# Projecting P and Q in two halves of TensorE's rows, and moving the places of nodes into a tile of differences

## The chip, the core and the metric

The kernel runs on one core of one Trainium2 chip. It is one program in one launch. The metric is the device time of that launch in microseconds (us), the median of several runs. The engines go by the names of the profile: PE (TensorE, with PEld for its weight loads), DVE (VectorE), ACT (ScalarE), POOL (GpSimd) and SP (SyncE, which issues the DMAs).

## What is computed

128 small graphs of 128 nodes with 64 features go through four residual layers, each after a layer norm and a maximum with zero. Almost all of the time goes to layer 0, a message over the edges:

```python
mask = (adj > 0.0).astype(x.dtype)
W1a, W1b = (W1[:F], W1[F:])
xj_proj = x @ W1a
diff = x[:, :, None, :] - x[:, None, :, :]
h = jax.nn.relu(xj_proj[:, :, None, :] + diff @ W1b + b1)
hm = jnp.einsum('bjkh,bjk->bjh', h, mask)
deg = jnp.sum(mask, axis=-1)
return hm @ W2 + deg[..., None] * b2
```

Here F is 64 and the hidden width H0 is 192. About an eighth of the entries of adj is not zero, and every node has an edge to itself. Layer 1 is three graph convolutions and an output projection, layer 2 is one convolution whose rows are normalized and then scaled by a mean and a variance over all nodes of all graphs, and layer 3 is a convolution followed by a small two-layer network.

## The kernel before

**Layer 0 as gathers.** For an edge from j to k the hidden value is relu(P[j] + Q[k]), where P = h (W1a + W1b) + b1 and Q = -h W1b. The kernel projects P and Q once for each node and then, instead of going over all 128 x 128 pairs, goes over the neighbours of each node: the i-th neighbour of all nodes in one task. Q is split into three bf16 parts whose sum is the fp32 value, and a one-hot matrix (`oh`, `ohn`) picks the rows of Q by matmuls that add onto P, which lies in PSUM already.

**Groups and pairs.** Four graphs (G) make a group, so there are 32 groups (NG). Two graphs (a pair p of NP = 2) share the 128 partitions when they are transposed: hT has 64 rows of features of the one and 64 of the other. Before the change the weights wp and wq are block diagonal, 128 rows by 2 x 192 columns with zeros in the off-diagonal blocks, so that one matmul of 128 rows and 384 columns projects both graphs of a pair. W is 384.

**Tasks.** A group has 20 tasks in layer 0 (ORDER). A near task (4 matmuls of 192 columns) covers one of three thirds of the nodes with all three parts of Q at once, a full task (12 matmuls) covers one neighbour of all nodes. The three tiles blk0 to blk2 in PSUM take turns: task t uses block t % 3. In each task `fill` copies P of the group into a block (ACT, L560), `differences` adds Q on PE (tile name blk), and DVE adds the positive part to acc (L583; the first tasks of a group are L579 and L581). `fill(t + 2)` and the one-hot of task t + 3 are written down after the first quarter of task t.

**PSUM.** There are eight banks. Each blk has two, of which columns 0 to 383 hold P and differences; 128 columns of each bank are spare. The spare columns hold ysum (blk0), ysq (blk1) and the degrees of nodes (`degs_at`, blk2), all set to zero at the start. The remaining two banks are the pool ps, from which `bank(name)` takes one in turn for everything else.

**Side work.** Between the half tasks of group g, two generators are advanced: `prepare(g + 1)` and `after_layer0(g - 1)`, which is `layer0_end` (tiles ps_sA, ps_sB, ps_o), `layer1` (ps_ah, ps_ag, ps_pr, t at L640) and `layer2_norm` (ps_ga, ps_pr, y at L654, sqy at L656, nrm). A planner in `network` chooses: each half task allows PACE us of PE work, by the estimate of `spend`, and a generator that lags behind its schedule by LAG steps runs anyway. N_PREPARE and N_AFTER are the numbers of steps. The framework then orders each engine's instructions, mostly as they are written down, with ready ones first, and adds the waits. It keeps two engines from one PSUM bank at a time by waits.

**prepare(g)**, in its order: transposed adjacency; ranks of neighbours (ps_rank, ps_rankT, leftT at L424); keys and `lower` (L441); the place of each node in an order by the number of its neighbours, from matmuls into ps_place, read by `to_b` (L452); hT (L328); Q (ps_q, the copies L465, the subtractions L466, the casts L467 and L468, the DMAs to q_dram and back into near_q); hs, the features in the new order (ps_ga); num (L482); degrees into degs_at, read by spare_n (L510); fro (L495); P (ps_p with its bias, copied to psort at L517), psort_r by DMA, and extra (L525).

All matmuls are recorded at L103, the transposes at L108, so the tile names tell them apart.

## Time and profile before

| | |
|---|---|
| runs | 1396.9, 1397.42 and 1404.55 us, median 1397.42 |
| profiled execution | 1398.05 us, its span 1396.2 |
| mean granted clock of TensorE | 0.979 |
| PE busy | 1232.2 us (88%) |
| DVE busy | 1167.8 us (84%) |
| ACT busy | 990.8 us (71%) |
| POOL busy | 270.6 us (19%) |
| ps_p, fp32 matmul passes | 128 records, 59.0 us busy |
| ps_q, fp32 matmul passes | 128 records, 52.5 us busy |

The span is the time from the first to the last instruction of one profiled execution. A busy time is the sum over which at least one instruction of the engine runs; matmuls are pipelined, so each lasts longer in the records than it keeps the next one off, and the spacing of their starts says more than their lengths. "Idle before" is the time in which an engine stood still ahead of a group of instructions, with the instruction that ended it. The chain is followed back from the last instruction, at each step to what released it; a piece of work that is not on it can still take part in the next longest chain.

### The profile page before, as it was taken

The numbers are of one execution on the slowest core, as the hardware profiler recorded it, in microseconds if no ns is written. First come the engines' busy times: TensorE is split into PE (matmuls) and PEld (weight loads), VectorE is DVE, ScalarE is ACT, GpSimd is POOL, SyncE is SP. The second block draws the span as 40 slices with busy tenths as digits, with TensorE's granted clock in tenths as the row PEclk, the third lists the DMA queues.
The fourth block names the chain that finished last, engine by engine and source line by source line (L and its number), as shares of the span: only waits on it lengthen the run. The fifth ranks groups of instructions, "written<-read, shape, count | busy, mean of one in ns | idle before, by whom it ended". The sixth has DMA issues, their size and how long they took to land.

```text
span 1396.2 us, 29319 instructions
## 1 busy us (share of the span) xinstructions
PE 1232.2 (88%) x10964; PEld 959.3 (69%) x10964; DVE 1167.8 (84%) x2629; ACT 990.8 (71%) x1883; POOL 270.6 (19%) x322
## 2 busy tenths in 40 slices
PE   3788999999999999999999999999999999995787
PEld 1467777777777777777777777776777777763566
DVE  6898888888888888888888888888898888866973
ACT  1677777777777777777777777777777777753783
POOL 3111111111111111111111111111111111015830
PEclk9899999999999999999999999999999999997889
DMA  5443222322323222222222222223222212200345
GB/s 120 131 120 98 67 66 78 83 83 84 83 76 83 84 75 75 76 63 75 66 78 84 83 84 83 75 83 84 76 75 79 62 59 60 76 9 15 93 112 126
DMA packets 108788, 110.97 MB, mean 79 GB/s; under 512 B 42895, under 2 KB 88220, under 8 KB 108636
## 3 DMA queue, kind: packets, MB, share of 16 engines
q1 hardware_dynamic: 108636, 109.00, 28.5%
q8 instruction: 89, 1.46, 0.5%
q14 instruction: 63, 0.52, 0.1%
HBM read 52.70 MB, written 35.29 MB: 63 GB/s over the span
## 4 chain that ended last, share of the span: by engine, by line
PE 65%; ACT 17%; DVE 13%; issue 2%; SPq 1%; DMA 1%; DVEq 0%; POOL 0%; ACTq 0%; POOLq 0%
PE blk L103 24%; PE ps_pr L103 10%; ACT blk L560 9%; DVE acc L583 6%; PE ps_ag L103 5%; PE ps_p L103 5%; PE ps_sA L103 5%; PE ps_o L103 3%; PE ps_sB L103 3%; PE ps_q L103 2%; PE ps_ah L103 2%; PE ps_hm L103 2%; ACT q L465 2%; DVE leftT L424 1%; PE ps_key L103 1%
## 5 line engine op out<-in xcount | busy, mean ns | idle before, releaser
L583 DVE SCALAR_TENSOR_TENSOR acc<-blk,acc 128x768 f32<-128x768 f32 x576 | 543.1, 950 | 65.0 <-PE blk L103 38.9
L560 ACT COPY blk<-psort 128x768 f32<-128x768 f32 x544 | 436.1, 806 | 134.1 <-DVE acc L583 132.2
L103 PE MATMUL blk<-q,oh 128*128 128x192 bf16 x3072 | 318.2, 246 | 34.5 <-ACT blk L560 34.3
L103 PEld LDWEIGHTS <-oh 128*128 128x128 bf16 x3072 | 259.1, 98 | 89.3 <-issue 84.3
L103 PE MATMUL blk<-near_q,ohn 128*128 128x192 bf16 x1536 | 199.7, 246 | 22.4 <-ACT blk L560 22.1
L103 PEld LDWEIGHTS <-ohn 128*128 128x128 bf16 x1536 | 134.7, 98 | 59.9 <-issue 45.3
L468 POOL TENSOR_TENSOR q<-rest,q 128x768 bf16<-128x768 f32 x32 | 52.8, 1648 | 209.1 <-ACT q L467 209.1
L642 POOL TENSOR_TENSOR adjT<-adjT,ident 128x512 f32<-128x512 f32 x32 | 41.9, 1310 | 254.8 <-PE ps_ag L103 254.8
L668 POOL TENSOR_TENSOR y<-y,nrm 128x256 f32<-128x256 f32 x32 | 19.7, 615 | 363.7 <-PE blk L103 238.1
L634 ACT COPY msg<-ps_pr 128x512 f32<-128x512 f32 x64 | 37.5, 586 | 68.9 <-PE ps_pr L103 67.5
L541 DVE TENSOR_SCALAR ohn<-near_n 128x1536 bf16<-128x1536 bf16 x128 | 84.3, 695 | 0.0
L103 PE MATMUL ps_pr<-g,dT 128*128 128x128 f32 x512 | 78.8, 288 | 0.8 <-ACT dT L626 0.8
L560 ACT COPY blk<-psort_r 128x768 f32<-128x768 f32 x96 | 77.5, 807 | 0.5 <-DVE acc L583 0.4
L103 PEld LDWEIGHTS ps_pr<-g,dT 128*128 128x128 f32 x512 | 64.3, 191 | 11.5 <-issue 7.2
L103 PE MATMUL ps_ag<-adjT,msg 128*128 128x128 f32 x512 | 71.5, 283 | 0.6 <-ACT msg L634 0.5
L103 PEld LDWEIGHTS <-ones_b 3*128 3x128 bf16 (+2 forms) x280 | 26.0, 93 | 59.1 <-issue 51.5
L103 PEld LDWEIGHTS ps_ag<-adjT,msg 128*128 128x128 f32 x512 | 62.1, 191 | 5.9 <-ACT msg L634 5.5
L103 PE MATMUL ps_p<-wp,hs 128*128 128x384 f32 x128 | 59.0, 543 | 0.0
L626 ACT ACTIVATE dT<-ps_ag 128x512 f32<-128x512 f32 x96 | 56.8, 592 | 3.0 <-PE ps_ag L103 2.8
L103 PE MATMUL ps_q<-wq,hT 128*128 128x384 f32 x128 | 52.5, 534 | 4.4 <-ACT hT L328 0.8
L103 PE MATMUL ps_hm<-ident,h 128*64 128x128 f32 x248 | 43.6, 308 | 14.0 <-ACT h L841 13.9
L103 PE MATMUL ps_sA<-fro,acc 128*128 128x128 f32 x256 | 53.3, 290 | 2.1 <-ACT dT L626 1.9
(220 smaller groups left out, 2544.8 us busy)
## 6 DMA issues: line engine op xcount, KB each, us to landing
q_dram<-q SPq DMA_DIRECT2D x32, 567.0 KB
near_q<-q_dram SPq DMA_DIRECT2D x96, 189.0 KB
near_n<-n_dram SPq DMA_DIRECT2D x96, 126.0 KB
a<-in_adj_dram SPq DMA_DIRECT2D x32, 256.0 KB
adjT_dram<-adjT SPq DMA_DIRECT2D x32, 256.0 KB
adjT<-adjT_dram SPq DMA_DIRECT2D x32, 256.0 KB
psort_r<-psort SPq DMA_DIRECT2D x32, 228.0 KB
fro_r<-fro SPq DMA_DIRECT2D x32, 152.0 KB
```

The lines of the kernel that those rows point to most:

```text
L103: return nc.tensor.matmul(o, w, x, **kw)
L424: nc.vector.scalar_tensor_tensor(flat(leftT), pk, float(NEAR), flat(mT), ALU.is_gt, ALU.mult)
L465: nc.scalar.copy(parts_q[:, 0, p, :], pq[:, 0:W])
L468: nc.gpsimd.tensor_tensor(parts_q[:, 2], rest, parts_q[:, 1], ALU.subtract)
L541: nc.vector.tensor_scalar(oh.rearrange("p t b n -> p (t b n)"), near_n[g % 2].rearrange("p t b n -> p (t b n)"), float(i + 1), None, ALU.i ...
L560: nc.scalar.copy(columns(t), psorts[g][in_segments(n)])
L583: nc.vector.scalar_tensor_tensor(acc, o, 0.0, acc, ALU.max, ALU.add)
L626: nc.scalar.activation(flat(dT), pa, AF.Relu)
L634: nc.scalar.copy(flat(msg), pm)
L642: nc.gpsimd.tensor_tensor(adjT, adjT, ident.unsqueeze(1).to_broadcast([P, G, P]), ALU.add)
L668: nc.gpsimd.tensor_tensor(y, y, over_f(nrm), ALU.mult)
```

## The change

P and Q are now projected by `projected`. wp and wq hold the same 64 x 192 weights twice, once in each half of the rows, without the zero blocks. Each fp32 matmul has 64 rows and 192 columns: half k of hT (or hs) against half k of the weights, into bank k, so that one bank holds the first graphs of both pairs and the other the second ones. `issue_after` fixes that the two halves alternate on PE. Both banks of the pool are taken at once. For P the two bias matmuls (3 rows, 384 columns) come first, one for each bank. The copies take one bank each, of the same size as before, with another layout of the destination; they all follow the matmuls at once, and the two steps that the pairs had become one step that counts as two.

The places of a group come into spare columns of blk1 (`places_at`) in place of a bank of their own; they are added onto the zeros set at the start. ysq leaves blk1: it takes the columns of the degrees in blk2, set to zero anew after the last group. The two memsets of the padded weights on POOL go. `spend` counts fp32 matmuls of 64 rows at half, and PACE goes from 0.85 to 0.82. The diff, without the blank lines that it adds:

```diff
--- before.py
+++ after.py
@@ -46,7 +46,7 @@
 ORDER = [kind[sum(k is kind for k in ORDER[:n])] for n, kind in enumerate(ORDER)]
 FIRST, FIRST_R = 0, ORDER.index((None, FULL))
 N_PREPARE, N_AFTER = 14, 26
-PACE, LAG = 0.85, 2.5
+PACE, LAG = 0.82, 2.5
 LATE = 18
 LASTS = 1.9
 PARTS = [2, 4, 6, 6, 6, 8]
@@ -94,7 +94,7 @@
         f32 = dtype == F32
         kind = (f32, tuple(w.shape), n)
         m = w.shape[-1]
-        one = max(0.026, 0.00043 * n) if not f32 else max(0.22, 0.0018 * n) * (0.5 if m == F and n == P else 1.0)
+        one = max(0.026, 0.00043 * n) if not f32 else max(0.22, 0.0018 * n) * (0.5 if m == F and n == P or w.shape[0] == F else 1.0)
         spent["us"] += one + (0.045 if kind != spent["kind"] else 0.0)
         spent["kind"] = kind
 
@@ -160,13 +160,12 @@
 
     w1, w2 = io["L0_gnn_W1"], io["L0_gnn_W2"]
 
-    wp = keep.tile([P, 2, H0], F32, name="wp")
-    wq = keep.tile([P, 2, H0], F32, name="wq")
-    wtop = setup.tile([P, 2, H0], F32, tag="wtop", name="wtop")
+    wp = keep.tile([P, H0], F32, name="wp")
+    wq = keep.tile([P, H0], F32, name="wq")
+    wtop = setup.tile([P, H0], F32, tag="wtop", name="wtop")
     for t, src in ((wtop, w1[0:F, :]), (wp, w1[F : 2 * F, :])):
-        nc.gpsimd.memset(t, 0.0)
         for k in range(2):
-            nc.sync.dma_start(t[k * F : (k + 1) * F, k, :], src)
+            nc.sync.dma_start(t[k * F : (k + 1) * F, :], src)
     nc.vector.tensor_scalar(wq, wp, -1.0, None, ALU.mult)
     nc.vector.tensor_tensor(wp, wp, wtop, ALU.add)
     w2a = keep.tile([P, F], F32, name="w2a")
@@ -252,9 +251,9 @@
             matmul(t[:, k * 512 : (k + 1) * 512], ones_b[0:3, :], rows3[:, 0:512], start=True, stop=True)
 
 
-    ysum, ysq = (t.rearrange("p (a n) -> p a n", a=2)[0:G, :, W:512] for t in blks[0:2])
-    degs_at = blks[2].rearrange("p (a n) -> p a n", a=2)[:, :, W:512]
-    for t in (ysum, ysq, degs_at):
+    behind_blk = [t.rearrange("p (a n) -> p a n", a=2)[:, :, W:512] for t in blks]
+    ysum, places_at, degs_at = behind_blk[0][0:G], behind_blk[1], behind_blk[2]
+    for t in (ysum, places_at, degs_at):
         nc.vector.memset(t, 0.0)
 
 
@@ -391,6 +390,32 @@
         nc.scalar.copy(flat(adjT), pt)
         nc.sync.dma_start(saved[g], flat(adjT))
         return adjT
+    def few(t, g):
+        half, at = divmod(g, NG // 2)
+        return t[:, half, at * 2 * G : (at + 1) * 2 * G]
+    def projected(ht, w, name, bias_row=None):
+        both = [bank(name) for _ in range(2)]
+        last = None
+        for k in range(2) if bias_row else ():
+            with tc.issue_after(last.ins) if last is not None else ExitStack():
+                last = matmul(both[k][:, 0:W].rearrange("p (a h) -> p a h", a=NP), ones_b[0:3, :], bias(bias_row, NP), start=True, stop=False, skip_group_check=True)
+        for p in range(NP):
+            for k in range(2):
+                half = slice(k * F, (k + 1) * F)
+                with tc.issue_after(last.ins) if last is not None else ExitStack():
+                    last = matmul(both[k][:, p * H0 : (p + 1) * H0], ht[half, p, :], w[half, :], start=bias_row is None, stop=True, skip_group_check=True)
+        return [t[:, 0:W].rearrange("p (a h) -> p a h", a=NP) for t in both]
+    def graphs(t, k):
+        return t[:, :, k * H0 : (k + 1) * H0]
 
     sorts, psorts, accs, loaded = {}, {}, {}, {}
 
@@ -444,9 +469,9 @@
         nc.vector.scalar_tensor_tensor(flat(rank), flat(rank_t), float(NEAR), flat(rank), ALU.min, ALU.add)
         nc.vector.tensor_copy(degs[:, :, 1], prv[:, :, P - 1])
         yield
-        pl = bank("ps_place")
-        for b in range(G):
-            matmul(pl[:, b : b + 1], lower[:, b, :], ones_b[:, 0:1], start=True, stop=True)
+        pl = few(places_at, g)
+        for b in range(G):
+            matmul(pl[:, b : b + 1], lower[:, b, :], ones_b[:, 0:1], start=False, stop=True, skip_group_check=True)
         next(ln)
         to_b = once.tile([P, G, P], BF16, tag="to_b", name="to_b")
         nc.vector.tensor_tensor(to_b, row_b.unsqueeze(1).to_broadcast([P, G, P]), pl[:, 0:G].unsqueeze(2).to_broadcast([P, G, P]), ALU.is_equal)
@@ -458,12 +483,11 @@
         hT = transposed(h, "0")
         yield
         rest = once.tile([P, NP, W], F32, tag="rest", name="rest")
-        for p in range(NP):
-            pq = bank("ps_q")
-            matmul(pq[:, 0:W], hT[:, p, :], flat(wq), start=True, stop=True)
-            yield
-            nc.scalar.copy(parts_q[:, 0, p, :], pq[:, 0:W])
-            nc.vector.tensor_tensor(rest[:, p, :], pq[:, 0:W], parts_q[:, 0, p, :], ALU.subtract)
+        pq = projected(hT, wq, "ps_q")
+        for k in range(2):
+            nc.scalar.copy(graphs(parts_q[:, 0], k), pq[k])
+            nc.vector.tensor_tensor(graphs(rest, k), pq[k], graphs(parts_q[:, 0], k), ALU.subtract)
+        yield 2
         nc.scalar.copy(parts_q[:, 1], rest)
         nc.gpsimd.tensor_tensor(parts_q[:, 2], rest, parts_q[:, 1], ALU.subtract)
         nc.sync.dma_start(q_dram[g], parts_q[0 : 3 * THIRD].rearrange("n q p c -> n q (p c)"))
@@ -484,8 +508,7 @@
         for q in range(3):
             nc.sync.dma_start(near_n[g % 2][q * THIRD : (q + 1) * THIRD].rearrange("r t b n -> r t (b n)"), n_dram[g].rearrange("(t r) c -> r t c", t=3))
         yield
-        half, at = divmod(g, NG // 2)
-        pd = degs_at[:, half, at * 2 * G : (at + 1) * 2 * G]
+        pd = few(degs_at, g)
         for b in range(G):
             matmul(pd[:, 2 * b : 2 * b + 2], to_b[:, b, :], degs[:, b, :], start=False, stop=True, skip_group_check=True)
         pf = bank("ps_fro")
@@ -510,12 +533,10 @@
         nc.vector.scalar_tensor_tensor(spare_n[:, g], pd.rearrange("p (b q) -> p b q", q=2), -1.0, caps.unsqueeze(1).to_broadcast([P, G, 2]), ALU.mult, ALU.add)
         yield
         psort = edge.tile([P, NP, W], F32, tag="psort", name="psort")
-        for p in range(NP):
-            pp = bank("ps_p")
-            matmul(pp[:, 0:W].rearrange("p (k h) -> p k h", k=2), ones_b[0:3, :], bias("L0_gnn_b1", 2), start=True, stop=False)
-            matmul(pp[:, 0:W], hs[:, p, :], flat(wp), start=False, stop=True)
-            nc.scalar.copy(psort[:, p, :], pp[:, 0:W])
-            yield
+        pp = projected(hs, wp, "ps_p", "L0_gnn_b1")
+        for k in range(2):
+            nc.scalar.copy(graphs(psort, k), pp[k])
+        yield 2
         psort_r = once.tile([P, NP, W], F32, tag="psort_r", name="psort_r")
         for n, start in zip(SEGS, STARTS):
             nc.sync.dma_start(psort_r[start : start + n], psort[0:n])
@@ -768,6 +789,8 @@
         return bank(name) if i == 0 else blks[i - 1][:, k * 512 : (k + 1) * 512]
 
     run(last)
+    ysq = degs_at[0:G]
+    nc.vector.memset(ysq, 0.0)
     for g in range(NG):
         y = ys[g]
         nc.vector.tensor_tensor(y, y, over_g(shift), ALU.subtract)
```

## Prediction

> **What bounds the kernel now.** I read the page's busy line, the busy time of the regular middle, the chain that ended last by line and then in order of time, and the timeline around each edited step. Busy line, then the stretch from 200 to 1150 us:
>
> ```profile
> PE 1232.2 (88%) x10964; PEld 959.3 (69%) x10964; DVE 1167.8 (84%) x2629; ACT 990.8 (71%) x1883; POOL 270.6 (19%) x322
> 200.00:1150.00 950.00, 874.30 (x7796) 685.92 (x7794) 830.68 (x1766) 713.53 (x1343) 157.14 (x176) 1.00 0.27 76
> ```
>
> In the middle PE is busy 874.3 of 950 us (92%), DVE 87%, ACT 75%. PE leads, but DVE is near, and a cut in PE's work is worth its full length only where the chain runs on PE. The place step L452 returns every 37.6 us on average, so there are 31 such periods and a first group before them. Chain by engine and line, then one period of it in order of time:
>
> ```profile
> PE 65%; ACT 17%; DVE 13%; issue 2%; SPq 1%; DMA 1%; DVEq 0%; POOL 0%; ACTq 0%; POOLq 0%
> PE blk L103 24%; PE ps_pr L103 10%; ACT blk L560 9%; DVE acc L583 6%; PE ps_ag L103 5%; PE ps_p L103 5%; PE ps_sA L103 5%; PE ps_o L103 3%; PE ps_sB L103 3%; PE ps_q L103 2%; PE ps_ah L103 2%; PE ps_hm L103 2%; ACT q L465 2%; DVE leftT L424 1%; PE ps_key L103 1%
> ```
>
> ```profile
> 610.69 0.44 DVE t L640
> ...
> 614.39 0.93 PE ps_q L103 x2
> 615.34 0.48 ACT q L465
> ...
> 623.76 1.11 PE ps_p L103 x3
> 626.63 1.11 PE ps_p L103 x3
> ```
>
> The reader is to see three things. Both projections of P are whole on the chain, 2 x 1.11 us. Of Q only the first half is (0.93); from there until 621.51 the chain runs over ACT and DVE. And at 610.69 it goes through t, a DVE read that has nothing to do with what PE does next, except that it frees a PSUM bank.
>
> **P.** An fp32 matmul appears as two passes. The timeline of PE has one projection of P like this:
>
> ```profile
> 623.52 0.24 PE L103 MATMUL blk<-degs,to_b 128*128 128x2 bf16 x4
> 623.69 0.33 PE L103 MATMUL ps_p<-rows,ones_b 3*128 3x384 bf16 x1
> 623.95 0.91 PE L103 MATMUL ps_p<-wp,hs 128*128 128x384 f32 x2
> 624.70 0.82 PE L103 MATMUL blk<-near_q,ohn 128*128 128x192 bf16 x8
> ```
>
> From bias to projection 0.26 us pass, though a 384-column bf16 stream alone takes 0.16 (192 columns start 0.08 apart): a switch between 3-row and 128-row weights costs 0.10. The two passes need 0.75: 2 x 0.3225, the spacing of passes within ps_q, and 0.11 for a first weight load that nothing covers. With 0.10 for entering the 3-row mode: 1.11.
> After the change one group has an entry 0.10, two bias matmuls 0.32, a switch to 64 rows 0.10, a bare first load 0.11, eight passes of 192 columns (0.161 each) in two banks of rows, and a switch back 0.10. Side by side the passes take 4 x 0.161 = 0.645, in all 1.38 against 2.22: **-0.84**. The trace holds no 64-row matmul[...].
> Do the halves run side by side? The nearest row is the other split, by columns:
>
> ```profile
> 618.91 0.66 PE L103 MATMUL ps_ga<-to,h 128*64 128x128 f32 x8
> 619.50 0.40 PE L103 MATMUL ps_num<-to_b,rank 128*128 128x128 bf16 x4
> ```
>
> Eight passes and a switch in 0.59 us, where eight full-width passes of 128 columns (0.11) would need 0.86: two at a time. [...] By the row 0.645[...]. I take the row, since both cases are two tiles of fp32, and keep 0.20 (no overlap at all) and 0.84 as ends.
>
> **Q.** PE's time falls from 0.11 + 4 x 0.3225 = 1.40 to 0.96 (0.10 + 0.11 + 0.645 + 0.10; the entry falls into the wait for hT that is there now). The path does not get shorter: the first copy now needs both pairs of graphs of its half, which end after 0.11 + 0.645, just when the first pair ended before. ACT's two copies (0.48 each), DVE's two subtractions (0.55) and all later casts are the same in number and size. The copies now follow each other with no fill (L560, 0.80) between, so one fill comes 0.48 later and PE's next differences with it; the second fill comes when it did. The last cast, POOL's subtraction (1.65) and the four DMAs behind it on SP (q_dram, three near_q) move one step, some 0.94 us, later; no near_q DMA appears among the waits of the middle, so their cover is the rest of the group; without it they would cost those 0.94. **0**, ends -0.2 and +0.3.
>
> **Places.** Four matmuls and their reader to_b stay, but leave the ring of two free banks (tag ps) for blk1. Around them now:
>
> ```profile
> 610.49 0.24 PE L103 MATMUL ps_place<-ones_b,lower 128*128 128x1 bf16 x4
> 610.53 0.80 ACT L560 COPY blk<-psort 128x768 f32<-128x768 f32 x1 [2.29 <-DVE acc L583]
> 611.03 0.95 DVE L583 SCALAR_TENSOR_TENSOR acc<-blk,acc 128x768 f32<-128x768 f32 x1
> 611.17 0.49 PE L103 MATMUL ps_o<-w2b,sB 128*128 128x128 f32 x2 [0.44 <-DVE t L640]
> 611.90 0.68 DVE L452 TENSOR_TENSOR to_b<-row_b,ps_place 128x512 bf16<-128x512 bf16 x1
> ```
>
> ps_o waits 0.44 for t because the banks alternate: ps_pr, place, ps_o. With place gone, ps_o gets the bank that lower read long before: **-0.44**.
> [...] 20 tasks a group over 3 blocks rotate the place through the ring. If blk1 is the task about to start, to_b ends (612.58) as its matmuls start: 0. If it is the next one, the place waits for the fill until 611.33, and ps_o starts 0.43 later than now. If it is the one just read, it waits for the accumulation until 611.98: 1.08 later. [...] The trace has the same construction in the degrees in blk2; idle time before them:
>
> ```profile
>   ACT blk L560: 3.7, 9
> ```
>
> 3.7 us over 32 groups are 0.12 each, as other matmuls are queued ahead. But its reader takes 0.15 us and to_b 0.68. I take **+0.25**, nearer the row; ends 0.12 and 0.50. What queues behind a late place on PE is ps_o, and behind to_b on DVE the next mean and accumulation.
>
> **Two banks at once.** P and Q each hold both free banks until their copies are done. For Q both were in turn used by it before. For P, ps_pr (L2's) is in the way:
>
> ```profile
> 625.10 0.39 ACT L656 ACTIVATE sqy<-ps_pr 128x256 f32<-128x256 f32 x1
> ```
>
> Its bank is free at 625.5, 1.8 us after P starts now; the second bias, and by the written order everything of P, waits for it, and ps_ah (625.54) must then wait for a copy of psort. Eight differences (0.67) and twelve more (1.0) can fill PE meanwhile. Ends 0 and 1.7; the nearest row is the 0.44 of ps_o: **+0.45**.
>
> **Given back.** In the period from 642 the stretch behind P runs over ACT (fills, four extras of 0.45) for 7.8 us, as long as PE's own in the period shown. Where that holds, a part of P's gain meets ACT: **+0.15**, ends 0 and 0.4.
>
> **Rest.** Two POOL memsets (0.5 each) go; POOL has memsets until 11 us and the first x lands at 23, so 0. In the first group ps_q and ps_p are 2.93 each on the chain at a lower clock; about 1 each goes: -2 once. The memset of ysq goes to the end, beside the shift subtractions: 0. PACE asks for 0.82 instead of 0.85 us of PE work per half task, about what the projections save; it moves steps by a half task and I cost it at 0, ends -0.3 and +0.3.
>
> **Sum.** -0.84 - 0.44 + 0.25 + 0.45 + 0.15 = -0.43 us a group, times 31 is -13.3, with -2 makes -15. The profiled execution took 1398.05 us (span 1396.2), 0.6 above the median 1397.42; from the median: **1382**, own range 1366 to 1392.
>
> **Rivals.**
> All of it arrives (no bank wait, place at 0.12, nothing given back): -1.16 x 31 - 2 = -38, 1359. For it speaks the 65% of the chain on PE; against it DVE's 87%, which would become 90%.
> It is eaten: waits of 0.9 a group in place of one of 0.44, near 1397.
> Slower, by the pair of banks: if ps_pr's bank holds P for the whole 1.7, the sum is +0.82 x 31 - 2 = +23, 1421; it decides from 0.9 us a group on. For it speaks sqy's late place on ACT, against it the twenty differences that can go first.
> The halves do not overlap: P saves 0.20, Q's first copy is late by 0.42; +0.63 x 31 = +20, 1417. The column halves speak against it.
>
> **Numbers.** A measurement here tells 0.5%, 7 us. Chances: main case 0.55, all of it 0.12, eaten 0.12, banks 0.13, no overlap 0.08. Faster 0.64 (main case but its upper edge, and all of it), same 0.15, slower 0.21. The range 1354 to 1412 leaves out about a tenth above and less below.
>
> **What would show it.** ps_q and ps_p as 192-column passes of 64 rows that start in pairs, eight within 0.65 to 0.75 us; PE busy lower by some 40 us, DVE and ACT as before; ps_o no longer behind t; a place or to_b that waits on L560 or L583 by no more than 0.25 us a group; a period near 37.1 us. Wrong would be passes 0.16 apart (no overlap), or PE idle before ps_p or ps_ah on sqy or psort of more than 0.9 us a group.

## The result and the profile after

The changed kernel takes 1469.23 us (median of 4 runs, 1464.07 to 1475.98) where the kernel before took 1398.38 us in the same session: a ratio of 1.050, with a 95% interval of 1.0447 to 1.0554. It was forecast to take 1382 us, in a range that ended at 1412. The profiled execution after took 1464.07 us with a span of 1462.2, and is 66.0 us longer than the profiled span of before, 1396.2. All readings of the two traces below are of these spans.

The busy line of the page after, and the stretch from 200 to 1150 us (its columns: length; busy time and instructions of PE, PEld, DVE, ACT and POOL; granted clock; DMA share; GB/s):

```profile
PE 1251.8 (86%) x11220; PEld 986.4 (67%) x11220; DVE 1163.7 (80%) x2630; ACT 1000.8 (68%) x1883; POOL 273.0 (19%) x320
200.00:1150.00 950.00, 846.07 (x7563) 672.50 (x7560) 777.87 (x1674) 682.94 (x1267) 151.87 (x168) 0.95 0.26 73
```

The third number from the end of the second line carries the news: the granted clock of TensorE in the regular middle is 0.95, where it was 1.00. PE is busy for 20 us longer than before although its work became less, and yet the shares of the span fell, PE's from 88 to 86%, DVE's from 84 to 80%, ACT's from 71 to 68%. So no engine became the bound. Something makes them wait for each other, and PE runs slower for part of the time.

The row of granted clock over 40 equal slices of the span, first of before, then of after:

```profile
PEclk9899999999999999999999999999999999997889
```

```profile
PEclk9999999899999999998999999998999999998799
```

A slice of 36 us that shows 8 in the middle of the run (the eighth, the nineteenth and the twenty-eighth) had a mean clock below 0.9, so more than a fifth of it was at half speed. Before, no such slice lies between the start and the last part. In the records of the clock behind this row there are 16 spells at half speed between 100 and 1220 us of after, 95.6 us together, each of 3.41, 6.83 or 10.24 us; before has none there.

The chain that ended last, by engine and by line:

```profile
PE 65%; ACT 16%; DVE 14%; issue 3%; POOL 1%; DMA 0%; SPq 0%; ACTq 0%; DVEq 0%; POOLq 0%
PE blk L103 25%; PE ps_pr L103 10%; DVE acc L604 7%; ACT blk L581 7%; PE ps_ag L103 6%; PE ps_sA L103 4%; PE ps_o L103 3%; PE ps_ga L103 3%; PE ps_sB L103 2%; PE ps_ah L103 2%; PE ps_hm L103 2%; PE ps_p L103 2%; PE ps_key L103 1%; PE ps_q L103 1%; DVE leftT L449 1%
```

P fell from 5% of the chain to 2%, Q from 2 to 1. The saving is there. The place of P was taken by the passes into the difference tiles (blk) and by DVE's accumulation (acc).

PE's own waits in the middle (200 to 1150 us), each with its total, how often, and the longest, first before, then after:

```profile
PE blk L103 <- ACT blk L560: 43.2, 78, 0.6
...
PE ps_o L103 <- DVE t L640: 11.0, 25, 0.4
```

```profile
PE blk L103 <- ACT blk L581: 59.4, 64, 1.8
PE ps_sB L103 <- DVE leftT L449: 14.5, 24, 0.6
PE ps_ga L103 <- DVE rest L489: 10.6, 16, 0.7
PE blk L103 <- DVE to_b L477: 6.8, 8, 0.8
PE ps_ah L103 <- ACT psort L538: 4.4, 16, 0.4
```

The wait of ps_o for t is gone, as forecast. In its place stand one for rest, one for to_b and one for psort, and above all longer waits for the refill L581: one of 1.8 us is half as long as the shortest spell (3.41 us), and the next part shows what that means. The timeline of PE from Q on, in one group:

```profile
605.13 0.59 PE L103 MATMUL ps_q<-wq,hT 64*128 64x192 f32 x2
605.65 0.25 PE L103 MATMUL blk<-ones_b,lower 128*128 128x1 bf16 x4
606.75 0.82 PE L103 MATMUL blk<-near_q,ohn 128*128 128x192 bf16 x8 [0.85 <-DVE to_b L477]
607.50 0.92 PE L103 MATMUL ps_q<-wq,hT 64*128 64x192 f32 x6
609.38 1.15 PE L103 MATMUL blk<-q,oh 128*128 128x192 bf16 x12 [0.96 <-ACT blk L581]
...
611.28 0.49 PE L103 MATMUL blk<-near_q,ohn 128*128 128x192 bf16 x4
613.43 0.24 PE L103 MATMUL blk<-degs,to_b 128*128 128x2 bf16 x4 [1.66 <-ACT blk L581]
...
615.63 1.22 PE L103 MATMUL ps_pr<-wbn,zT 128*128 128x128 f32 x4
616.79 0.50 PE L103 MATMUL ps_p<-rows,ones_b 3*128 3x384 bf16 x1
...
617.35 2.13 PE L103 MATMUL blk<-q,oh 128*128 128x192 bf16 x12
619.41 0.50 PE L103 MATMUL ps_p<-rows,ones_b 3*128 3x384 bf16 x1
619.83 1.60 PE L103 MATMUL ps_p<-wp,hs 64*128 64x192 f32 x8
```

Three things are to be seen. First, the halves work: at full clock the starts of the two passes of a pair lie 6 to 7 ns apart, and the next pair follows 0.155 us later (0.26 behind the first pair). Second, both projections are torn apart by the wait for their second bank. Q's first matmul, into the one bank, stands alone at 605.13 with its two passes one after the other (0.27 us apart); the other six passes follow at 607.50, as two pairs and two single passes that have no partner left. The first bias of P stands at 616.79, the second at 619.41. Third, from 614.4 PE's passes take about twice as long: twelve that took 1.15 take 2.13 (their starts lie 0.160 apart in place of 0.082), and P's eight take 1.60 where Q's six took 0.92.

What Q waits for is on DVE:

```profile
606.01 0.69 DVE L477 TENSOR_TENSOR to_b<-row_b,blk 128x512 bf16<-128x512 bf16 x1 [0.78 <-PE blk L103]
...
606.95 0.41 DVE L631 TENSOR_TENSOR x<-x,ps_o 128x256 f32<-128x256 f32 x1
```

The read of ps_o (x) ends at 607.36 and is what the profile names as the release of Q's remaining weight loads. It stands on DVE behind to_b, and to_b waits for the place, which now lies in a difference tile. In all 24 groups of the middle Q's first matmul stands alone; in 16 of them the rest starts within 0.15 us of the end of this read. Q then takes 2.72 us from its first pass to its last, on average. With the places in their own bank (own_place below) Q is torn in none of 25 groups and takes 0.92.

The same stretch of after in windows of 3.41 us on the grid on which the clock changes: the 46 clock records of after start whole multiples of 3.4133 us apart, to within 1 ns (columns: length, PE busy with instructions, granted clock, DMA share, GB/s):

```profile
604.13:607.54 3.41, 2.56 (x29) 1.00 0.00 0
607.54:610.95 3.41, 2.45 (x27) 1.00 0.00 0
610.95:614.36 3.41, 1.68 (x25) 1.00 0.09 32
614.36:617.77 3.41, 3.41 (x19) 0.51 0.62 202
617.77:621.18 3.41, 3.41 (x20) 0.50 0.74 179
621.18:624.59 3.41, 3.35 (x25) 0.99 0.77 163
```

The window before the spell held 1.68 us of PE work, because of the idle 1.66 ahead of L581. It is followed by two windows at half speed in which PE is never idle, and then by full speed. Of the 16 windows that came before a spell in the middle of after, 14 held 1.72 us of busy time or less (the other two 1.96 and 2.08); of the 284 windows at full speed with no spell behind them, none held less than 1.73. In before the least busy of 328 windows had 2.05. These figures are the changed kernel's and no constant: where P's halves ran alone (p_halves below) spells also followed windows with 2.0 to 2.6 us on the same measure, so the profile's busy time alone does not tell when the clock falls.

**Where 66 us went.** With the spans cut at the to_b of groups 3 and 30 and at the first ps_sB, the account is this. A group takes 39.64 us where it took 37.62: over the 27 periods +54.5. The first ps_sB starts at 89.0 in place of 80.6: +8.4. The rest is +3.1. Within the periods, those without a spell (the kernel goes through the same three lengths in turn, as three blocks serve twenty tasks a group) add up to 115.2 us for three groups, against 112.76 before, which is +0.82 a group or 22 us; what remains, 1.2 a group or 33 us, comes with 3.29 us at half speed a group. The split of the periods is an estimate: two of the three lengths stand without a spell only in the first groups, and a spell can also move the groups after it.

The price of half speed can be read in a second way, without any edit, from executions of one and the same kernel, because they differ in it. The clock records of before and after show no other clock than 1.00 and 0.50, so half speed over the whole span is 2 x (1 - mean granted clock) x span. The four executions of the changed kernel have 140, 155, 156 and 171 us of it, with spans of 1462.2, 1466.7, 1468.2 and 1474.2: a line through them rises by 0.39 us of time for each us. Of the seven other kernels below with over 1 us of half speed a group, six rise by 0.35 to 0.49 and one (filler) does not rise; over the executions of all twenty kernels, each against the mean of its own, it is 0.24. The kernel before has 56 us of half speed on average, nearly all at its start and end. So the changed kernel has about 100 us more, and at 0.24 to 0.4 they are worth 24 to 40 of the 71 us. This too is an estimate, from few points, but the 33 us of the regular middle lie within it.

### The profile page after: what moved, and what is told of

Read it like the earlier page. It is cut to its first block, busy times and chain, and to the rows that moved or that the text cites. A ratio compares the mean times of both kernels' runs of the same rounds, so it can differ in the third digit from the quotient of the medians.

```text
span 1462.2 us, 29758 instructions
## 1 busy us (share of the span) xinstructions
PE 1251.8 (86%) x11220; PEld 986.4 (67%) x11220; DVE 1163.7 (80%) x2630; ACT 1000.8 (68%) x1883; POOL 273.0 (19%) x320
## 4 chain that ended last, share of the span: by engine, by line
PE 65%; ACT 16%; DVE 14%; issue 3%; POOL 1%; DMA 0%; SPq 0%; ACTq 0%; DVEq 0%; POOLq 0%
PE blk L103 25%; PE ps_pr L103 10%; DVE acc L604 7%; ACT blk L581 7%; PE ps_ag L103 6%; PE ps_sA L103 4%; PE ps_o L103 3%; PE ps_ga L103 3%; PE ps_sB L103 2%; PE ps_ah L103 2%; PE ps_hm L103 2%; PE ps_p L103 2%; PE ps_key L103 1%; PE ps_q L103 1%; DVE leftT L449 1%
## 5 line engine op out<-in xcount | busy, mean ns | idle before, releaser
L581 ACT COPY blk<-psort 128x768 f32<-128x768 f32 x544 | 435.4, 805 | 161.4 <-DVE acc L604 150.0
L103 PE MATMUL blk<-q,oh 128*128 128x192 bf16 x3072 | 344.9, 254 | 46.4 <-ACT blk L581 46.3
L103 PEld LDWEIGHTS <-oh 128*128 128x128 bf16 x3072 | 266.2, 101 | 94.3 <-issue 87.8
L103 PE MATMUL blk<-near_q,ohn 128*128 128x192 bf16 x1536 | 211.0, 252 | 34.3 <-ACT blk L581 26.4
L689 POOL TENSOR_TENSOR y<-y,nrm 128x256 f32<-128x256 f32 x32 | 22.7, 709 | 436.4 <-PE blk L103 166.5
L581 ACT COPY blk<-psort_r 128x768 f32<-128x768 f32 x96 | 77.7, 809 | 0.0
L103 PE MATMUL ps_pr<-g,dT 128*128 128x128 f32 x512 | 72.0, 284 | 0.4 <-ACT dT L647 0.4
L562 DVE TENSOR_SCALAR ohn<-near_n 128x1536 bf16<-128x1536 bf16 x128 | 67.9, 559 | 0.0
L103 PE MATMUL ps_q<-wq,hT 64*128 64x192 f32 x256 | 47.8, 374 | 4.4 <-ACT hT L327 4.4
L300 ACT ACTIVATE sq<-xc 128x256 f32<-128x256 f32 x96 | 39.9, 416 | 15.3 <-DVE xc L297 14.4
```

The costliest lines, as they stand in the source:

```text
L103: return nc.tensor.matmul(o, w, x, **kw)
L300: nc.scalar.activation(sq, xc, AF.Square)
L562: nc.vector.tensor_scalar(oh.rearrange("p t b n -> p (t b n)"), near_n[g % 2].rearrange("p t b n -> p (t b n)"), float(i + 1), None, ALU.i ...
L581: nc.scalar.copy(columns(t), psorts[g][in_segments(n)])
L689: nc.gpsimd.tensor_tensor(y, y, over_f(nrm), ALU.mult)
```

## The experiments

All were run in rounds with the kernel before on the same chip; ratios are to that kernel, with 95% intervals. "Half speed" is the time at the halved clock in a group, mean of groups 3 to 30; the kernel before has none, the changed kernel 3.29 us.

| run | us | ratio | period, us | half speed, us |
|---|---|---|---|---|
| own_place | 1419.6 | 1.0164 (1.0139 to 1.0190) | 38.14 | 1.26 |
| places_only | 1400.0 | 1.0024 (1.0010 to 1.0038) | 37.61 | 0.25 |
| pace85 | 1435.8 | 1.0281 (1.0262 to 1.0300) | 38.71 | 1.14 |
| both_banks | 1446.6 | 1.0351 (1.0306 to 1.0397) | 39.15 | 2.15 |
| own_place85 | 1442.4 | 1.0342 (1.0311 to 1.0372) | 38.81 | 1.14 |
| p_halves | 1468.6 | 1.0508 (1.0491 to 1.0526) | 39.85 | 3.41 |
| q_halves | 1404.8 | 1.0057 (1.0029 to 1.0084) | 37.91 | 1.52 |
| filler | 1434.3 | 1.0284 (1.0251 to 1.0317) | 38.68 | 1.14 |
| before_fill | 1407.8 | 1.0065 (1.0044 to 1.0086) | 38.05 | 0 |
| own_fill | 1408.3 | 1.0069 (1.0046 to 1.0091) | 37.73 | 0 |
| q_fill | 1392.9 | 0.9958 (0.9941 to 0.9976) | 37.29 | 0.13 |
| p_early | 1429.6 | 1.0213 (1.0190 to 1.0235) | 38.48 | 0.76 |
| p_early_fill | 1440.3 | 1.0305 (1.0272 to 1.0337) | 38.74 | 0 |
| own_early_fill | 1416.3 | 1.0120 (1.0090 to 1.0151) | 37.96 | 0.25 |
| before_early | 1400.1 | 1.0011 (0.9995 to 1.0027) | 37.67 | 0 |
| q_fill82 | 1409.2 | 1.0075 (1.0053 to 1.0098) | 37.88 | 0 |
| p_split_fill | 1437.4 | 1.0290 (1.0253 to 1.0328) | 38.83 | 0.38 |
| q_split_fill | 1383.7 | 0.9908 (0.9892 to 0.9925) | 36.99 | 0.13 |

### The change taken apart

**own_place**: the changed kernel with the places back in a bank of the ring.

```
-        pl = few(places_at, g)
+        pl = bank("ps_place")
...
-            matmul(pl[:, b : b + 1], ..., start=False, ...)
+            matmul(pl[:, b : b + 1], ..., start=True, ...)
```

> The changed kernel, with the places back in a bank of the pool of two (ps_place), all else as changed. Places theory (their matmuls and to_b tie PE to the ring of blocks, the pauses that follow let the clock fall): 1385 to 1397, no half-clock spells in the middle. Banks theory (P and Q hold both free banks at once): 1450 or more, spells stay. Planner theory (PACE 0.82 and the new costs order the work badly): 1450 or more.

It took 1419.6 us, between the forecasts, so none of the three theories fits. Beside the halves the moved place costs 50 us. Half speed falls from 3.29 to 1.26 us a group without it, and Q is in one piece again. Over all executions half speed falls from 156 to 87 us, which at 0.24 to 0.4 is 17 to 28 of the 50 us.

**places_only**: the kernel before with the places in the spare columns of blk1 and nothing else.

> The kernel before, with only the places moved to the spare columns of blk1 (and ysq to those of blk2). Places theory: 1440 or more, with half-clock spells. Banks theory: 1383 to 1397, since the wait of 0.44 us for the bank before ps_o goes and a wait of 0.12 to 0.5 comes. Planner theory: the same as banks theory.

1400.0 us, 3 above the nearer forecast: by itself the move is worth nothing and costs nothing that matters. The stage from ps_sB to ps_hT became 1.73 us shorter in a group (5.89 in place of 7.62), the two from Q to ps_fro 1.24 us longer together, and the others 0.45 longer together. What the place saves comes back within the same group, in a stretch that waits for ACT and DVE. The 50 us are thus no price of the place, but of the place together with the halves. The trace of after shows where the two meet: to_b stands ahead of the read of ps_o on DVE, and Q, which now needs both banks at once, waits for that read.

**pace85**: the changed kernel with PACE .85 as before.

> The changed kernel with PACE 0.85 as before. Planner theory: below 1400. Places theory and banks theory: 1450 to 1480, since their waits do not depend on it.

1435.8 us, so PACE .82 costs the changed kernel 34 us. Again neither forecast was met. The opposite holds with the places in the ring:

**own_place85**: own_place with PACE .85.

> The changed kernel with the places back in their own bank and PACE 0.85. Banks theory (holding both free banks at once costs what the halves save): 1405 to 1430, as with PACE 0.82 (1419.6). Planner theory: 1397 or less.

1442.4 us, 23 us more than with .82, and above both forecasts. A step of 0.03 us in how work is released moves the time by more than any cost in the forecast's sum, and with either sign.

**p_halves** and **q_halves**: own_place85 with only one of the two projections in halves. The other has its block-diagonal weights and its loop over pairs back.

```
-        pq = projected(hT, wq, "ps_q")
...
+        for p in range(NP):
+            pq = bank("ps_q")
+            matmul(pq[:, 0:W], hT[:, p, :], flat(wqf), start=True, stop=True)
...
```

> Only P in halves into both banks; Q as before with block-diagonal weights, pair by pair; places in their own bank, PACE 0.85. If Q's single step does the harm (the first pass takes one bank and waits for the other, both copies stand together in ACT's queue ahead of the fills, the stretch from Q to fro grows): 1375 to 1392, P's 0.84 us a group with little lost. If every joint holding of both banks does: 1405 or more.

> Only Q in halves into both banks; P as before, pair by pair; places in their own bank, PACE 0.85. If Q's single step does the harm: 1405 to 1425, with the stretch from Q to fro longer than the 6.3 us of before. If P's does: 1390 to 1400.

P's halves alone take 1468.6 us, as much as the whole change; Q's alone 1404.8. The harm is P's, at this PACE and with the places in their own bank. The two do not add up: both together (own_place85) take 26 us less than P's alone.

**both_banks**: the kernel before, full 128-row matmuls and no halves, but both pairs of Q issued together into two banks with the copies behind them, and P likewise.

```
-        for p in range(NP):
-            pp = bank("ps_p")
+        pp = [bank("ps_p") for _ in range(NP)]
+        for p in range(NP):
...
-            yield
+        yield 2
```

> The kernel before, with 128-row block-diagonal matmuls as they were, but both pairs of P and of Q projected at once into both banks and copied after, in one step that counts as two; places in their own bank, PACE 0.85. Banks theory: 1440 or more without any 64-row matmul. Places theory and planner theory: 1390 to 1410, a few waits for a bank more.

1446.6 us, 3.5% slower without a single 64-row matmul, and at 2.15 us of half speed a group. Its like with the halves is own_place85 (the same PACE, the places in their own bank), at 1442.4 us: what the halves themselves add to the pair of banks is 4 us of gain. Most of the loss thus comes from how the projection takes its banks and its place among the steps, not from rows of TensorE.

### The clock

**filler** and **before_fill**: the changed kernel, and the kernel before, with the four matmuls of ps_num issued four more times, into the same columns. They add 0.89 us a group on PE (ps_num takes 1.22 in place of 0.33), about 28 us in all, at a place where it tends to be idle.

```
+        for _ in range(4):
+            for b in range(G):
+                nc.tensor.matmul(pn[:, b * P : (b + 1) * P], rank[:, b, :], to_b[:, b, :], start=True, stop=True)
```

> The changed kernel with the four matmuls of ps_num issued five times over, each time with the same result: 0.88 us of PE work more in every group, 28 us in all, put where PE waits for the fills behind Q. If the fall of the clock in windows of low activity is what costs most: fewer half-clock spells and a time of 1430 to 1460 in spite of more work. If the clock is a symptom only: 1469 to 1497.

> The kernel before, with the four matmuls of ps_num issued five times over: 28 us of PE work more in all. It has no half-clock spells in the middle, so the work can only cost: 1405 to 1427. This is the price of the filler where the clock has nothing to gain.

The changed kernel became 35 us faster for being given more to do. The regular middle of filler:

```profile
200.00:1150.00 950.00, 864.66 (x8190) 697.35 (x8189) 797.45 (x1722) 700.05 (x1300) 155.60 (x174) 0.99 0.27 74
```

The clock is 0.99, and half speed 1.14 us a group in place of 3.29. Over all executions it falls from 156 to 76 us, which at 0.24 to 0.4 explains 19 to 32 of the 35 us; the rest can lie in the order, as 56 of 6890 matmuls of groups 6 to 28 changed places. The same repeats cost the kernel before about 9 us, but there its order changed more (375 of 6732), so this is not the plain price of the work.

**own_fill** and **q_fill**: own_place with the same repeats, and q_halves with two repeats in place of four.

> The changed kernel with places in their own bank (1419.6 without filler), ps_num five times over. Clock theory: the spells (1.26 us a group, some 0.4 of which are lost, 15 us) go and the filler costs less than where it has no spells to remove: 1400 to 1420. Clock as a symptom: 1430 to 1447.

> Only Q in halves (1404.75; its periods without a spell are 37.26 us against 37.60 before), ps_num three times over, 14 us of PE work. Clock theory: spells gone, 1385 to 1397. Clock as a symptom: 1405 to 1419.

q_halves and q_fill are the clearest evidence for the clock. PE, ACT, DVE and POOL run the same instructions in the same order in groups 6 to 28, the repeats aside, and a period without a spell is as long (37.26 and 37.24 us). Only half speed differs, 1.52 and 0.13 us a group, and the kernel with more work is 12 us faster.

own_fill has no spell left in the middle and takes 1408.3 us, as before_fill (1407.8). This pair shows the two halves at equal clock, though the two differ in PACE as well: a group takes 37.73 against 38.05 us, 8.6 less over 27 periods, and the start gives it back (the first ps_sB stands at 89.2 against 80.8). q_fill, at 1392.9 us, is a little below the kernel before.

### The bank of ps_pr

This is one group of p_halves, with DVE, ACT and PE together:

```profile
618.59 0.40 ACT L680 COPY y<-ps_pr 128x256 f32<-128x256 f32 x1
...
618.76 0.32 PE L103 MATMUL ps_p<-rows,ones_b 3*128 3x384 bf16 x1 [0.18 <-ACT fro L523]
...
619.59 0.80 ACT L586 COPY blk<-psort 128x768 f32<-128x768 f32 x1 [0.60 <-DVE acc L609]
...
620.32 0.38 ACT L682 ACTIVATE sqy<-ps_pr 128x256 f32<-128x256 f32 x1
...
620.44 0.64 PE L103 MATMUL blk<-near_q,ohn 128*128 128x192 bf16 x3 [1.36 <-ACT blk L586]
...
621.01 0.50 PE L103 MATMUL ps_p<-rows,ones_b 3*128 3x384 bf16 x1
...
621.44 1.01 PE L103 MATMUL ps_p<-wp,hs 64*128 64x192 f32 x4
...
622.38 2.10 PE L103 MATMUL blk<-q,oh 128*128 128x192 bf16 x12
...
624.41 1.01 PE L103 MATMUL ps_p<-wp,hs 64*128 64x192 f32 x4
```

The first bias finds a free bank at 618.76. The second needs the one that sqy reads until 620.70, and sqy stands on ACT behind a refill, which waited for DVE. PE runs dry for 1.36 us, the passes behind it run at half clock (twelve at 622.38 take 2.10 us where they take 1.15 at full), and the projection ends at 625.4, 6.7 us after it began. **p_early** lets sqy read y's copy in SBUF, so that ps_pr's bank is free after the copy of y. **before_early** is the control: the kernel before with this edit alone.

```
-        nc.scalar.activation(sq.rearrange("p b f -> p (b f)"), pyf, AF.Square)
+        nc.scalar.activation(sq.rearrange("p b f -> p (b f)"), yf, AF.Square)
```

> Only P in halves (1468.57), with layer 2's square sqy read from the copy y in SBUF in place of ps_pr, so that the bank that P's second half waits for is free one ACT instruction (0.4 us and what is queued between) earlier. If the wait for that bank is what P's joint holding costs: the stretch from fro to ah gets shorter by 0.5 us or more and the time falls to 1420 to 1455. If P's harm lies elsewhere: 1460 to 1475.

> The kernel before with the square of y taken from its copy in SBUF: a control. If ps_pr's bank is no wait of the kernel before, the edit by itself moves nothing: 1393 to 1403 us. If the edit is a gain for any order of the work, it gains here too: below 1390 us, and what it gave to P's halves says nothing of the pair of banks.

p_early took 1429.6 us, 39 less than p_halves; before_early 1400.1, no gain. The gain is therefore one that only a kernel with the pair of banks has, as the slower rival of the forecast said. But the wait does not cost its own length: from the first bias to the second it is 2.35 us in p_halves and 0.21 in p_early, on average, while periods without a spell stayed about as they were (38.3 and 38.2 us). Most of the 39 us come in the periods with spells: half speed fell from 3.41 to 0.76 us a group. The edit also lets other work of PE change places, so that the wait alone made the spells is likely and not shown.

### What is left at full clock

**p_early_fill** and **own_early_fill** were to take away both, the long wait and the spells.

> P's halves alone, with the square of y taken from its copy in SBUF and the matmuls of ps_num issued four times more. Theory A (all that P's halves cost is the wait for ps_pr's bank and the half-speed spells): both are now taken away, so the saving of P's passes is left, 1385 to 1405 us. Theory B (two projections that take both banks at once cost time of their own, by the order in which their copies and the banks' next users then stand): 1415 to 1435 us, near the 1429.6 us without the repeats, at a granted clock of .98 or more.

> Both projections in halves, places in a bank of their own, PACE .82, the square of y from SBUF, the matmuls of ps_num issued four times more. The same without the SBUF read took 1408.3 us. Theory A: the wait for ps_pr's bank was left in it, and goes: 1385 to 1398 us. Theory B: the taking of both banks by each projection is left: 1403 to 1412 us.

Theory A fell, for both, and both lie above the range of theory B too. own_early_fill is 8 us slower than own_fill, so where the clock is up, reading y early gains nothing. p_early_fill takes 1440.3 us at no half speed in these groups, and a group 38.74 us against 38.05 of before_fill. The account of PE's busy and idle time in a group, made from the start and end of every matmul of groups 3 to 29 (busy time is the union, so that each matmul counts from the end of the one before it):

| us a group | before_fill | p_early_fill | own_fill | q_split_fill |
|---|---|---|---|---|
| P (ps_p) | 2.21 | 1.48 | 1.43 | 2.21 |
| Q (ps_q) | 1.56 | 1.52 | 0.85 | 0.92 |
| differences (blk) | 13.62 | 14.19 | 13.95 | 13.40 |
| ps_ag and ps_ah | 3.67 | 4.10 | 4.07 | 3.87 |
| all other busy | 14.15 | 14.11 | 14.13 | 13.93 |
| idle | 2.84 | 3.38 | 3.29 | 2.58 |
| period | 38.06 | 38.79 | 37.72 | 36.90 |

(q_split_fill, told below, has two repeats and not four.) P's saving is there, 0.73 us a group, close to the forecast's. It is spent again on the same engine: the 152 passes into the difference tiles take 0.57 longer, ps_ag and ps_ah 0.43, and PE is idle for 0.54 more. The median pass into the difference tiles did not become longer (246 ns in both). These passes stand in more stretches (21.3 a group in place of 20.0) with more breaks inside (8.1 in place of 6.3), and four passes in one stretch take 0.49 us where twelve take 1.15, so each restart counts about 0.16 as busy beside 0.083 a pass. In the timeline of p_early_fill:

```profile
605.05 0.33 PE L103 MATMUL ps_p<-rows,ones_b 3*128 3x384 bf16 x1
606.38 0.41 PE L103 MATMUL blk<-near_q,ohn 128*128 128x192 bf16 x3 [0.99 <-ACT blk L589]
606.72 0.33 PE L103 MATMUL ps_p<-rows,ones_b 3*128 3x384 bf16 x1
606.98 0.60 PE L103 MATMUL ps_p<-wp,hs 64*128 64x192 f32 x4
607.50 1.16 PE L103 MATMUL blk<-q,oh 128*128 128x192 bf16 x12
608.60 0.60 PE L103 MATMUL ps_p<-wp,hs 64*128 64x192 f32 x4
609.13 0.59 PE L103 MATMUL blk<-near_q,ohn 128*128 128x192 bf16 x5
609.94 1.09 PE L103 MATMUL ps_ah<-adjT,h 128*65 128x128 f32 x8 [0.23 <-ACT psort L546]
```

The second bias still comes 1.67 after the first, because the copy of y now stands behind the same refill on ACT, which waited for DVE. The wait that p_early had removed (0.21) is back with the repeats (1.60 on average), so p_early_fill tests the clock and not the wait. In the kernel before the first pair of P's wide matmuls ran in just this stretch and covered it.

**p_split_fill** and **q_split_fill** let other work in between the two copies, as the kernel before does: a yield behind each of P's copies, and one ahead of each copy of Q, in place of the `yield 2` behind them. For Q it is this:

```
         for k in range(2):
+            yield
             nc.scalar.copy(graphs(parts_q[:, 0], k), pq[k])
...
-        yield 2
```

> p_early_fill (P's halves alone, square of y from SBUF, matmuls of ps_num four times more, 1440.3 us) with other work let in between the two copies of P out of its banks, as the kernel before lets it in between its two. Theory C (two copies in a row hold up ScalarE's refills of the difference tiles, and so TensorE's passes into them): 1400 to 1425 us. Theory D (both banks are taken by one projection, and the second copy now frees its bank later still): 1442 to 1465 us.

> q_fill (Q's halves alone, PACE .85, matmuls of ps_num two times more, 1392.9 us) with other work let in ahead of each of the two copies of Q, as in the kernel before. Theory C (copies in a row hold up the refills): 1378 to 1389 us, which would be clearly below both kernels. Theory D (banks held longer): 1395 to 1412 us.

For P nothing changed (1437.4 us, between the two forecasts): what it loses, it has lost before its copies. For Q it gained 9 us, to 1383.7 us, **0.9% below the kernel before**, the fastest of all versions. PE's waits in q_fill, then in q_split_fill:

```profile
PE blk L103 <- ACT blk L590: 28.5, 26, 1.1
PE ps_ga L103 <- DVE rest L493: 17.5, 26, 0.7
...
```

```profile
PE blk L103 <- ACT blk L590: 27.7, 26, 1.1
PE ps_sB L103 <- DVE leftT L453: 15.1, 25, 0.6
PE ps_o L103 <- DVE t L670: 11.4, 26, 0.4
PE ps_sA L103 <- ACT dT L656: 1.9, 8, 0.2
```

The wait of ps_ga for rest is gone. In the trace the two casts of Q still follow each other on ACT; what moved is the cast of rest behind them, which now lets one more refill go first. So the theory of copies in a row was right in the size and not in the detail.

**q_fill82**: q_fill with PACE .82 and four repeats.

> Q's halves alone with PACE .82 and the matmuls of ps_num issued four times more. If the slower release of work under .82 only matters through the clock, it adds the price of the two further repeats to the 1392.9 us of PACE .85 with two: 1393 to 1400 us. If PACE orders the work between the projections, as the two versions with places in a bank of their own had it (23 us less under .82), it is 1370 to 1388 us.

1409.2 us, above both theories, at no half speed, and 16 more than q_fill, where two more repeats would be some 4 to 5. PACE therefore acts with the clock at full speed too, by the order of the work, and .82 was the wrong side for this version.

**Still open.** Why P's halves alone cost 0.7 us a group at full clock, while P and Q in halves together with PACE .82 gain 0.3 (own_fill), is not settled: they differ in PACE too, and no run held P's pair while leaving the order of the other steps as it was. The waits in the trace make the order around P's two banks the likely cause; that is argued, not shown.

## Why the prediction was wrong

Three steps failed. Holding both banks at once was priced at 0.45 us a group for P and at nothing for Q; alone, without halves, it made the kernel 49 us slower (both_banks). PACE was put at 0 and moved the changed kernel by 34 us. And no term of the sum had the clock, through which much of both losses came: by the estimate above 24 to 40 of the 71 us. The saving of work that the sum began with was real. The terms one by one:

**P, -0.84.** Right as a saving of work: 2.21 to 1.43 us of PE in own_fill, -0.78. The halves do run side by side (starts 6 to 7 ns apart, 0.155 us a pair), so the row of column halves was the right one to go by, and the rival without overlap fell. (Its working leaves out the -2 of the start that the other rivals have, 1415 and not 1417; nothing hangs on it.) The 0.10 for each change of rows was the author's estimate from one spacing of the trace before; after shows about as much: 0.26 us from a bias to the first 64-row pass, and 0.255 from the last pass of a projection to the next full-row pass, 0.10 more than between pairs (medians at full clock). In the changed kernel itself P takes 1.69 us a group, as a part of it runs at half clock.

**Q, 0.** PE's own time fell by 0.71 a group (1.56 to 0.85, own_fill) where the working had 0.44; in the changed kernel, where Q is torn, by 0.15 alone (to 1.41). That the path would not get shorter held only for the copies where the change had put them: with the clock kept up Q's halves gained 6 us (q_fill), and with the steps behind its copies spread, 13 (q_split_fill). What was said of the copies (one fill comes later, up to +0.3) was the right size; q_split_fill got back 9 us, 0.3 a group, but by a refill that goes ahead of the cast of rest, not between the two copies.

**Places, -0.44 + 0.25.** The upper end of 0.50 is the mean of the working's three cases (0, 0.43 and 1.08), an estimate from the timeline of before. Both terms were found. ps_o no longer waits for t, and the place waits 6.8 us over the middle for to_b, 0.27 a group. Their sum does not reach the time: places_only is 0.24% slower, not 0.4% faster. The failed step is to book a wait removed from the chain as time saved while the next stretch hangs on ACT and DVE. Of what queues behind a late to_b the working named the next mean and accumulation, and not the read of ps_o, for whose bank Q waits.

**Two banks at once, +0.45.** The step that failed by its size. It priced one wait of P by the nearest wait in the trace, and for Q it said that both banks were used in turn before, at no price. The sign that it named did not show: PE idles before ps_ah for psort 4.4 us in the middle, 0.18 a group, and the profile names sqy in no wait of PE there. What did show is that a projection which holds one bank and waits for the other is torn: blk passes stand between its parts, ACT's refills come late, and PE runs dry for more than a microsecond. The rival "slower, by the pair of banks" had the place right, sqy's reading of ps_pr's bank (p_early and before_early), and its 23 us for the whole change were nearer than the main case. But it had the wait cost its own length on PE's path, and in p_halves most of the 39 us came with half speed. Q's wait for the bank of ps_o it did not name.

**Given back, +0.15.** Named, and much too small. In own_fill, the kindest case, blk, ps_ag and ps_ah take 0.73 us a group more and idle time 0.45, 1.2 together, against a saving of 1.5 in P and Q.

**PACE, 0 within 0.3.** 0.3 a group is 9 us; it moved the changed kernel by 34 and own_place by 23 the other way. Why the sign turns is open.

**The start, -2 once.** It became +8.4. Without the POOL memsets the four loads of wtop and wp no longer wait, and SP issues them first (0.75 us instead of 7.80). The loads of the bias rows move behind others, from 7.7 to 14.2 us. The six matmuls that set up the difference tiles from these rows then stand at 22.4 instead of 16.3, and the first group's adjacency work queues behind them:

```profile
22.44 2.74 PE L103 MATMUL blk<-rows,ones_b 3*128 3x512 bf16 x6
```

The step "two POOL memsets go, 0" looked only at POOL and at the arrival of x. It did not follow the other loads on SP's queue. In all versions with the new weights the first Q starts about 4 us later (34.3 in place of 30.4). That is half of the 8.4 us. The other half comes behind P of the first groups: with Q's halves alone (q_halves, q_fill) the first ps_sB stands at 83.0 and 81.7 us, with P's alone (p_halves) at 87.9, and 80.6 before.

**The clock.** No step of the sum had it, and by the estimates above it is one of the largest items. The profile of before showed a clock of 1.00 and least busy windows of 2.05 out of 3.41 us. It could not show what follows a thinner window, as it holds no spell in the middle. The sum took each wait as costing its own length. In the changed kernel each of the 16 windows that pauses had thinned to 1.58 to 2.08 us of work was followed by 3.41 to 10.24 us at half speed.

## What to carry to other kernels

Work taken from the leading engine is only worth what the engine behind it lets through: book it against the stretch in which it falls, and ask whether it was covering somebody's wait there. A step that needs two buffers of a ring of two holds up everything else that uses the ring, from its first allocation to its last copy, and it is safer to price that whole interval than the last wait in it: list who reads each of the two buffers last, and what stands ahead of that reader on its engine. Where TensorE's work is thinned out, look at the least busy stretches of a few microseconds: in this kernel windows with a pause of 0.85 to 1.83 us stood ahead of 3.41 to 10.24 us at half clock, and 28 us of added work shortened the run by 35.

## What was not expected of the hardware

- The clock halved behind windows of 3.41 us that were half busy: 1.58 to 2.08 us of busy time in the windows before the 16 spells of the middle, with a longest pause of 0.85 to 1.83 us in them.
- Two 64-row fp32 tiles of TensorE overlap almost fully: starts 6 to 7 ns apart and 0.155 us a pair of 192-column passes, so that four pairs (0.62) do what four full-row passes of 384 columns did at 0.3225 each (1.29).
- More PE work in less time: 28 us of repeats, 35 us gained; and 12 us gained by fewer repeats in an order of work that stayed the same (q_fill against q_halves).
